# The x3 stage of a four-layer kernel: factor rows in two tiles, x2 loads issued behind the x3 store, gate product in the gate's tile

## Chip, cores and metric

The kernel runs on one core of a Trainium2 chip. The metric is the device time of one execution in microseconds (us); the kernel before took 3424.25 us, the median of 3 runs (3423.7 to 3426.99). PE is the engine for matrix products, DVE the vector engine, ACT the engine for functions, POOL the general one, SP the engine that issues most of the DMAs here.

## The reference, cut to what matters

Four layers act on an image of 256 x 256 tokens with 128 channels (D), each as x = x + layer(gn(x)). The change lies in the end of layer 2, the triangle multiplication. Cut to that:

```python
zn = layernorm(gn(x), ln_in_w, ln_in_b)
a = sigmoid(zn @ Wga + bga) * (zn @ Wla + bla)
b = sigmoid(zn @ Wgb + bgb) * (zn @ Wlb + blb)
k = einsum('bimc,bmjc->bijc', a, b)
out = sigmoid(zn @ Wgo + bgo) * (layernorm(k, ln_o_w, ln_o_b) @ Wlo + blo)
x3 = x + out
```

The group norm of layer 3 needs the sum and the sum of squares of each channel of x3, so these are taken on the way.

## The kernel before, in words

Data stays channel-major between the stages: x2T, kD and x3T are DRAM arrays of 128 rows (channels) by 65536 tokens. A chunk is SC = 2048 tokens, 1 MB in float32, and there are NSC = 32 chunks. Three stages bear on the change:

- The stage that makes a and b (L1101 to L1235) leaves the factor 1/sqrt(var + eps) of every token in rs2D, and the gates of the last two chunks (30 and 31) in tiles of their own, `gates`.
- The triangle product (L1257 to L1294) goes over the 128 channels in 32 groups of four. For each group SP issues the store of k, the loads of the next a and b, and in the last three groups a load of x2 (`load7x`, chunks 0 to 2).
- The x3 stage (L1300 to L1398) goes over the 32 chunks. The order of its instructions on every engine is the order of the program (`manual_schedule`).

One step s of the x3 stage, as it is written:

- `load7k(s + 3)` (L1309): the load of k for chunk s + 3 into one of 4 tiles.
- `load7x(s + 5)` (L1254, L1255): the load of x2 for chunk s + 5 and of its factor row, 2048 numbers into one partition of the tile rs2. Seven tiles hold x2: three from one pool, four from another. Chunk s + 5 takes the tile of chunk s - 2, so its load waits until the x3 store of chunk s - 2 has landed. The row of chunk s takes partition 32 * (s % 4), so four rows are held.
- For each half h of 1024 tokens:
  - `gate7(s + 3, h)`: PE multiplies x2 by the gate's weight (L1329), DVE adds a column and multiplies by the broadcast factors into the tile p7_zg, of which there are two (L1339, "the gate product"), ACT takes the sigmoid into the gate tile p7_g, of which there are five (L1340). So chunk s + 3 uses the gate tile of chunk s - 2.
  - PE multiplies the normalised k by the output weight (L1329), and DVE adds a bias and multiplies by the gate, into the gate tile (L1383, "the second product").
  - In the first half PE spreads the factors of k for chunk s + 1 (L1087), and POOL broadcasts the factor row of chunk s + 4 to all partitions, into one of two tiles (`spread_z`, L1323).
  - DVE multiplies k of chunk s + 1 by its factors (L1318).
- POOL adds the product to x2, in the x2 tile (L1396). In the last chunk DVE does it (L1389).
- `finish7(s - 1)`: ACT takes the sum and the sum of squares of x3 of chunk s - 1 (L1343, L1344). Both write their full output, which nobody reads, into the gate tile of chunk s - 1. SP stores x3 (L1349).

The profile leaves digits out of names: p_x is p7_x, p_zg is p7_zg, p_g is p7_g, p_k is p7_k, p_rb is the broadcast factor, p_rk the spread factors of k, p_pm the PSUM tiles of the products, and rs__17908 the tile of the factor rows. A wait is set by the framework from the tiles: who first writes into a reused tile waits for the last users of what was there.

Of the kernel before, what the change touches and what calls it, by code (L numbers as in the profile page):

```python
# [9 lines left out]
F32 = mybir.dt.float32  # L10
AF = mybir.ActivationFunctionType
# [5 lines left out]
P = 128  # L17
# [3 lines left out]
SC = 2048  # L21
NSC = T // SC
# [10 lines left out]
def kernel(ctx: ExitStack, tc: tile.TileContext, a: dict, out: bass.AP):  # L33
    nc = tc.nc
# [22 lines left out]
    rs2D = dram.tile([1, T], F32, name="rs2D")  # L57
# [89 lines left out]
    b2w = const.tile([P, 6], F32, name="b2w")  # L147
# [91 lines left out]
    with tc.tile_pool(name="x0", bufs=1) as xres, tc.tile_pool(name="p0", bufs=3) as sb:  # L239
        held = {s: xres.tile([P, SC], F32, name=f"x0_{s}") for s in range(RES, NSC)}  # L240
        with tc.tile_pool(name="p0ps", bufs=3, space=PSUM) as ps, tc.tile_pool(
            name="f0ps", bufs=2, space=PSUM
# [167 lines left out]
        with tc.tile_pool(name="p1", bufs=2) as wk_sb, tc.tile_pool(  # L410
            name="p1ps", bufs=4, space=PSUM
# [70 lines left out]
    with tc.tile_pool(name="p2e", bufs=6) as eb, tc.tile_pool(name="p2c", bufs=1) as cs:  # L482
        triT = cs.tile([P, NH, 2, N], F32, name="triT")
        with tc.tile_pool(name="p2", bufs=2) as sb, tc.tile_pool(
            name="p2S", bufs=2, space=PSUM
        ) as psS, tc.tile_pool(name="p2z", bufs=1, space=PSUM) as psZ, tc.tile_pool(
            name="p2M", bufs=3, space=PSUM
# [361 lines left out]
    with x1_scope:  # L849
        with tc.tile_pool(name="p3", bufs=3) as sb, tc.tile_pool(  # L850
            name="p3ps", bufs=3, space=PSUM
# [41 lines left out]
        with tc.tile_pool(name="z", bufs=2) as sb, tc.tile_pool(  # L893
            name="zps", bufs=3, space=PSUM
# [28 lines left out]
            at = turn_z(0)  # L923
            for k in range(16):
                nxt = turn_z(k + 1)
                pz = tri_multiply(nc, ps, at, AB[k // 2][1], k % 2).rearrange("p t n -> p (t n)")
                at = nxt
# [32 lines left out]
        with tc.tile_pool(name="p4", bufs=3) as sb, tc.tile_pool(  # L960
            name="p4psg", bufs=2, space=PSUM
        ) as psg, tc.tile_pool(name="p4psz", bufs=2, space=PSUM) as psz, tc.manual_schedule():
            zs, gts, sums = {}, {}, []
# [42 lines left out]
            for i, s in enumerate(order):  # L1006
# [14 lines left out]
                for h in range(2):  # L1021
                    hs = slice(h * 2 * CK, (h + 1) * 2 * CK)
# [57 lines left out]
    H2 = 2 * CK  # L1080
# [157 lines left out]
    rk_pool = rs2_scope.enter_context(tc.tile_pool(name="rk", bufs=1))  # L1238
    x7_pool = rs2_scope.enter_context(tc.tile_pool(name="x7", bufs=3))
    rk = rk_pool.tile([P, CK], F32, name="rk")  # L1240
    rs2 = rk_pool.tile([P, SC], F32, name="rs2_")

    def row7(s):
        at = 32 * (s % 4)
        return rs2[at : at + 1, :]

    k1 = rk_pool.tile([P, 2 * N], F32, name="k1")
    k2 = rk_pool.tile([P, 2 * N], F32, name="k2")
# [2 lines left out]
    def load7x(s, pool, bufs):  # L1251
        if s < NSC:
            xs7[s] = pool.tile([P, SC], F32, name="p7_x", bufs=bufs)
            nc.sync.dma_start(xs7[s], x2T[:, s * SC : (s + 1) * SC])  # L1254
            nc.sync.dma_start(row7(s), rs2D[:, s * SC : (s + 1) * SC])  # L1255

    with tc.tile_pool(name="p6", bufs=3) as sb, tc.tile_pool(name="p6ps", bufs=3, space=PSUM) as ps:  # L1257
        nc.vector.memset(k1, 0.0)
        nc.gpsimd.memset(k2, 0.0)  # L1259
        with tc.manual_schedule():  # L1260
            quads = {}

            def load6(q):
                if q < D // 4:
                    A = sb.tile([P, 4, 2 * N], F32, name="p6_A")
                    nc.sync.dma_start(A, aD[:, 4 * q : 4 * q + 4, :])
                    B = sb.tile([P, 4, 2 * N], F32, name="p6_B")
                    nc.sync.dma_start(B, bD[:, 4 * q : 4 * q + 4, :])
                    quads[q] = A, B

            def turn6(c):
                return tri_turn(nc, ps, sb, quads[c // 4][0], c % 4, ident, nc.vector.tensor_copy)

            for q in range(3):
                load6(q)
            at = turn6(0)
            for c in range(D):
                q = c // 4
                if c % 4 == 0:
                    K = sb.tile([P, 4, 2 * N], F32, name="p6_K")  # L1280
                nxt = turn6(c + 1) if c + 1 < D else None
                pz = tri_multiply(nc, ps, at, quads[q][1], c % 4).rearrange("p t n -> p (t n)")
                at = nxt
                nc.scalar.copy(K[:, c % 4, :], pz)  # L1284
                sq = sb.tile([P, 2 * N], F32, name="p6_sq")
                nc.scalar.activation(sq, pz, AF.Square)  # L1286
                nc.vector.tensor_tensor(k1, pz, k1, ALU.add)  # L1287
                nc.gpsimd.tensor_tensor(k2, k2, sq, ALU.add)  # L1288
                if c % 4 == 3:
                    nc.sync.dma_start(kD[4 * q : 4 * q + 4, :].rearrange("c (p t) -> p c t", p=P), K)  # L1290
                    del quads[q]
                    load6(q + 3)
                    if q >= D // 4 - 3:
                        load7x(q - (D // 4 - 3), x7_pool, 3)  # L1294
# [5 lines left out]
    with tc.tile_pool(name="p7", bufs=2) as sb, tc.tile_pool(name="p7psX", bufs=2, space=PSUM) as psX, tc.tile_pool(  # L1300
        name="p7psM", bufs=2, space=PSUM
    ) as psM, tc.manual_schedule():
        ks, rks, rbs, gts = {}, {}, {}, dict(gates)
        AHEAD = 3

        def load7k(s):
            if s < NSC:
                ks[s] = sb.tile([P, SC], F32, name="p7_k", bufs=4)
                nc.sync.dma_start(ks[s], kD[:, s * SC : (s + 1) * SC])  # L1309

        def spread_k(s):
            if s < NSC:
                rks[s] = broadcast_rows(psX, rk, s, "p7_rk")

        def normalise_k(s, h):
            if s < NSC:
                hs = slice(h * H2, (h + 1) * H2)
                nc.vector.tensor_tensor(ks[s][:, hs], rks[s][h], ks[s][:, hs], ALU.mult)  # L1318

        def spread_z(s):  # L1320
            if s < NSC and s not in gates:
                rbs[s] = sb.tile([P, SC], F32, name="p7_rb")
                nc.gpsimd.partition_broadcast(rbs[s], row7(s))  # L1323

        def product7(src, w, h):
            pm = psM.tile([P, 2, CK], F32, name="p7_pm")
            for c in range(2):
                k = 2 * h + c
                nc.tensor.matmul(pm[:, c, :], lhsT=w, rhs=src[:, k * CK : (k + 1) * CK], start=True, stop=True)  # L1329
            return pm.rearrange("p c t -> p (c t)")  # L1330

        def gate7(s, h):
            if s < NSC and s not in gates:
                hs = slice(h * H2, (h + 1) * H2)
                if h == 0:
                    gts[s] = sb.tile([P, SC], F32, name="p7_g", bufs=5)
                pg = product7(xs7[s], wf2[:, 4, :], h)
                zg = sb.tile([P, H2], F32, name="p7_zg")
                nc.vector.scalar_tensor_tensor(zg, pg, gcol, rbs[s][:, hs], ALU.add, ALU.mult)  # L1339
                nc.scalar.activation(gts[s][:, hs], zg, AF.Sigmoid, bias=b2w[:, 4:5])  # L1340

        def sums7(x, junk, i):
            nc.scalar.activation(junk, x, AF.Identity, bias=m2neg, accum_out=g1[:, i : i + 1])  # L1343
            nc.scalar.activation(junk, x, AF.Square, bias=m2neg, accum_out=g2[:, i : i + 1])  # L1344

        def finish7(s):
            x = xs7.pop(s)
            sums7(x, gts.pop(s), s)
            nc.sync.dma_start(x3T[:, s * SC : (s + 1) * SC], x)  # L1349

        load7k(0)
        load7x(3, sb, 4)
        spread_z(0)
        spread_z(1)

        nc.vector.scalar_tensor_tensor(k1, k1, -1.0 / D, k1, ALU.mult, ALU.mult)
        nc.vector.tensor_tensor(k2, k2, k1, ALU.add)
        nc.vector.tensor_scalar(k2, k2, 0.0, None, ALU.max)
        nc.scalar.activation(k2, k2, AF.Sqrt, bias=epst, scale=1.0 / D)
        nc.vector.reciprocal(k1, k2)  # L1360
        nc.sync.dma_start(rkD.rearrange("o (p t) -> p (o t)", p=P), k1)
        for c in range(4):
            nc.sync.dma_start(rk[32 * c : 32 * c + 32, :], rkD.rearrange("o (s c t) -> c (o s) t", c=4, t=CK)[c])
        for s in range(1, 3):
            load7k(s)
        load7x(4, sb, 4)
        for s in range(3):
            gate7(s, 0)
            gate7(s, 1)
            if s < 2:  # L1370
                spread_z(s + 2)
        spread_k(0)
        normalise_k(0, 0)
        normalise_k(0, 1)
        for s in range(NSC):
            load7k(s + 3)
            load7x(s + 5, *((x7_pool, 3) if (s + 5) % 7 < 3 else (sb, 4)))
            last = s == NSC - 1
            for h in range(2):
                hs = slice(h * H2, (h + 1) * H2)  # L1380
                gate7(s + AHEAD, h)
                pl = product7(ks[s], w2[:, 5, :], h)
                nc.vector.scalar_tensor_tensor(gts[s][:, hs], pl, b2w[:, 5:6], gts[s][:, hs], ALU.add, ALU.mult)  # L1383
                if h == 0:
                    spread_k(s + 1)
                    spread_z(s + AHEAD + 1)
                normalise_k(s + 1, h)
                if last:
                    nc.vector.tensor_tensor(xs7[s][:, hs], xs7[s][:, hs], gts[s][:, hs], ALU.add)  # L1389
                    if h == 0:  # L1390
                        finish7(s - 1)
                    sums7(xs7[s][:, hs], gts[s][:, hs], s + h)
                    nc.sync.dma_start(x3T[:, s * SC + h * H2 : s * SC + (h + 1) * H2], xs7[s][:, hs])
            del ks[s]
            if not last:
                nc.gpsimd.tensor_tensor(xs7[s], xs7[s], gts[s], ALU.add)  # L1396
                if s:
                    finish7(s - 1)  # L1398

# [483 lines left out]
```

## Time and profile before

| what | value |
|---|---|
| median of 3 runs | 3424.25 us |
| the profiled execution, device time | 3423.35 us |
| its span, first to last instruction | 3421.6 us |
| mean granted PE clock | 0.956 |
| triangle product, 2349 to 2640 us | 291 us, PE busy 289.81 |
| x3 stage up to its first store, 2640.0 to 2674.4 us | 34.4 us, PE busy 28.71, DMA 345 GB/s |
| x3 stage, first steps, 2674.4 to 2701.2 us | 26.8 us, PE busy 26.80, DMA 316 GB/s |
| x3 stage, further steps, 2701.2 to 2958.5 us | 257.3 us, PE busy 204.72, DVE 166.38, ACT 144.18, POOL 150.53, DMA 271 GB/s |
| x3 stage, last steps without gates, 2958.5 to 2997.5 us | 39.0 us, PE busy 22.96 |

The span is the time from the first to the last instruction; some 1.75 us of the device time lie outside of it. "Busy" is the time in which an engine worked; a clock of 1.00 is full speed. A group line shows who wrote what from what, the busy time of the group, the mean of one instruction, and then the idle time of that engine just before it with what ended that idle time. A wait line names the waiting instruction, then what ended its wait. Lines with SPq are DMA issues by SP.

### The profile page before, as it was taken

The page shows a single profiled execution, that of the slowest core. Times are in us where ns is not written, and L with a number is a line of the kernel's source. Part 1 is how long each engine was busy: PE and PEld are TensorE (multiplying, and loading weights), DVE is VectorE, ACT ScalarE, POOL GpSimd, SP SyncE. Part 2 cuts the span into 40 slices and gives each one's busy share as a digit, 9 for nine tenths or more (in the row PEclk, how much of TensorE's full clock was granted, in tenths as well). Part 3 has the DMA queues.
Part 4 walks back from the last instruction along what each step waited for, and adds up shares of the span by engine and source line. Part 5 has one row for each costly group of instructions (what it writes and reads, how often), then busy time and mean ns, then how long its engine had stood idle before and what let it go on. Part 6 is the DMA issues. An engine that isn't in the chain of part 4 may idle for free. (4 is left out here: it accounts for less than half of the span.)

```text
span 3421.6 us, 52156 instructions
## 1 busy us (share of the span) xinstructions
PE 3105.4 (91%) x20036; PEld 1648.5 (48%) x20036; DVE 2273.1 (66%) x2613; ACT 2021.0 (59%) x2209; POOL 1659.4 (48%) x904
## 2 busy tenths in 40 slices
PE   5669999999999999967996999999999987759998
PEld 5415555555555555524332444446997332224444
DVE  5627888888888888853555444554555766647776
ACT  3566777777777777734685454443444555626665
POOL 4045777777777777711581000002555655513443
PEclk7889999999999999989998999999999999979999
DMA  9982333333333333378697676767998877756764
GB/s 359 353 312 91 108 120 108 118 115 110 119 107 119 109 122 107 107 308 313 232 403 287 233 301 270 257 246 273 351 351 330 303 270 276 279 163 195 206 198 134
DMA packets 297913, 749.50 MB, mean 219 GB/s; under 512 B 74553, under 2 KB 145163, under 8 KB 248475
## 3 DMA queue, kind: packets, MB, share of 16 engines
q1 hardware_dynamic: 289723, 735.50, 60.4%
q0 software_dynamic: 7648, 9.55, 0.8%
q8 instruction: 161, 2.64, 0.3%
q10 hardware_dynamic: 288, 1.05, 0.1%
q14 instruction: 93, 0.76, 0.1%
HBM read 458.35 MB, written 287.64 MB: 218 GB/s over the span
## 5 line engine op out<-in xcount | busy, mean ns | idle before, releaser
L565 DVE TENSOR_TENSOR p_e<-p_S,triT 128x1024 f32<-128x1024 f32 x512 | 609.5, 1212 | 144.2 <-PE p_S L555 144.2
L575 POOL TENSOR_TENSOR p_es<-p_e 128x1024 f32<-128x1024 f32 x256 | 603.7, 2372 | 123.9 <-issue 65.1
L573 ACT ACTIVATE p_e<-p_e,mbT 128x1024 f32<-128x1024 f32 x512 | 552.0, 1138 | 59.8 <-DVE p_e L565 59.7
L1172 PE MATMUL p_pm<-p_zn,wf 128*128 128x512 f32 x1040 | 449.1, 593 | 2.2 <-ACT p_a L1207 1.9
L540 PE MATMUL p_mm<-p_xn,w 128*128 128x512 f32 x768 | 404.7, 610 | 0.3 <-DVE p_v L535 0.3
L1172 PEld LDWEIGHTS p_pm<-p_zn,wf 128*128 128x128 f32 x1040 | 196.7, 190 | 254.7 <-issue 246.5
L555 PE MATMUL p_S<-p_q,p_k 32*128 32x256 f32 x4096 | 294.9, 400 | 3.5 <-DVE p_e L565 3.3
L1579 POOL TENSOR_TENSOR p_q<-p_q,p_pb 128x2024 f32<-128x2024 f32 x32 | 144.1, 4503 | 252.0 <-DVE p_pb L1573 243.5
L555 PEld LDWEIGHTS p_S<-p_q,p_k 32*128 32x128 f32 x4096 | 185.7, 184 | 159.5 <-PE p_mm L531 91.7
L1843 PE MATMUL tp_z<-p_B,tp_at 128*128 128x256 f32 x1024 | 250.7, 388 | 0.7 <-DMA p_B<-bD 0.5
L514 POOL TENSOR_TENSOR p_xn<-p_xn,p_rs 128x1024 f32<-128x1024 f32 x63 | 151.2, 2400 | 204.9 <-DMA p_rb<-rzD 114.1
L588 PE MATMUL p_o<-p_e,p_v 128*32 128x256 f32 x4096 | 247.6, 382 | 0.0
L1259 POOL MEMSET k<- 128x512 f32 x1 | 0.5, 519 | 504.9 <-DVE p_zn L1165 504.9
L1288 POOL TENSOR_TENSOR k<-k,p_sq 128x512 f32<-128x512 f32 x128 | 162.9, 1273 | 159.1 <-ACT p_sq L1286 159.1
L1843 PEld LDWEIGHTS tp_z<-p_B,tp_at 128*128 128x128 f32 x1024 | 185.1, 191 | 22.6 <-DVE tp_at L1834 1.5
L1329 PE MATMUL p_pm<-p_x,wf 128*128 128x512 f32 x240 | 131.2, 677 | 58.8 <-DMA p_x<-x2T 52.6
L540 PEld LDWEIGHTS p_mm<-p_xn,w 128*128 128x128 f32 x768 | 125.8, 190 | 104.1 <-issue 88.1
L1287 DVE TENSOR_TENSOR k<-tp_z,k 128x512 f32<-128x512 f32 x128 | 88.5, 692 | 126.8 <-ACT p_sq L1286 126.8
L588 PEld LDWEIGHTS p_o<-p_e,p_v 128*32 128x32 f32 x4096 | 120.0, 109 | 109.3 <-ACT p_g L546 41.5
L1284 ACT COPY p_K<-tp_z 128x512 f32<-128x512 f32 x128 | 74.9, 585 | 157.6 <-PE tp_z L1843 157.6
L546 ACT ACTIVATE p_g<-p_mm,bgh 128x512 f32<-128x512 f32 x128 | 87.9, 687 | 131.3 <-PE p_mm L540 131.2
L531 PEld LDWEIGHTS p_mm<-w,p_xn 128*128 128x128 f32 x1024 | 134.4, 191 | 61.1 <-issue 60.4
(380 smaller groups left out, 5966.4 us busy)
## 6 DMA issues: line engine op xcount, KB each, us to landing
p_x<-x2T SPq DMA_DIRECT2D x60, 1024.0 KB
x<-x1T SPq DMA_DIRECT2D x51, 1024.0 KB
p_x<-in_x_dram SPq DMA_DIRECT2D x32, 1024.0 KB
p_x<-xT SPq DMA_DIRECT2D x64, 512.0 KB
x2T<-x SPq DMA_DIRECT2D x32, 1024.0 KB
aD<-p_a SPq DMA_DIRECT2D x32, 1024.0 KB
bD<-p_b SPq DMA_DIRECT2D x32, 1024.0 KB
p_A<-aD SPq DMA_DIRECT2D x32, 1024.0 KB
```

The lines of the kernel that those rows point to most:

```text
L514: nc.gpsimd.tensor_tensor(xn, xn, groups[g]["rs"], ALU.mult)
L531: nc.tensor.matmul(pm[:, k * D : (k + 1) * D], lhsT=t["xn"][:, b * P : (b + 1) * P], rhs=wf[:, 2 * D : 3 * D], start=True, stop=True,)
L540: nc.tensor.matmul(pm, lhsT=w, rhs=t["xn"][:, cs_], start=True, stop=True)
L555: nc.tensor.matmul(Ss[h // 2][:, h % 2, u, :], lhsT=t["k"][hp, r * N + u * P : r * N + (u + 1) * P], rhs=t["q"][hp, r * N : (r + 1) * N], ...
L565: nc.vector.tensor_tensor(e[:, :, 2 * p : 2 * p + 2, :].rearrange("p u h n -> p h u n"), Ss[p], triT[:, 2 * p : 2 * p + 2, :, :], ALU.add,)
L573: nc.scalar.activation(e[:, u, :, :], e[:, u, :, :], AF.Exp, bias=mbT[:, u, i : i + 1])
L575: nc.gpsimd.tensor_tensor(es, e[:, 0, :, :], e[:, 1, :, :], ALU.add)
L588: nc.tensor.matmul(t["o"][hp, r % 2, :], lhsT=t["v"][:, r * 2 + u, hp], rhs=e[:, u, h, :], start=(u == 0), stop=(u == 1),)
L1172: nc.tensor.matmul(pm[:, c, :], lhsT=wf2[:, i, :], rhs=zns[s][:, k * CK : (k + 1) * CK], start=True, stop=True)
L1288: nc.gpsimd.tensor_tensor(k2, k2, sq, ALU.add)
L1579: nc.gpsimd.tensor_tensor(q[:, :, 1 : N - 2], q[:, :, 1 : N - 2], pb[:, :, 0 : N - 3], ALU.add)
L1843: nc.tensor.matmul(pz[:, t, :], lhsT=at[:, u, t * P : (t + 1) * P], rhs=Bc[:, u, :], start=(u == 0), stop=(u == 1))
```

## The change

It has three parts, all of them in the x3 stage:

1. The factor rows get two tiles instead of one, so eight rows are held. Their loads are taken out of `load7x` and made by `load_row7`: rows 0 to 5 at the start of the triangle product, then row s + 6 at the start of step s. Rows of the chunks 30 and 31, whose gates exist already, are no longer loaded.
2. The x2 load of chunk s + 5 is issued at the end of step s, behind the x3 store of chunk s - 1. Before, it was issued near the step's start, in front of that store.
3. The gate product is written into the gate tile, and ACT takes the sigmoid in place. The tiles p7_zg are gone.

```diff
-    rs2 = rk_pool.tile([P, SC], F32, name="rs2_")
+    rs2 = [rk_pool.tile([P, SC], F32, name=f"rs2_{i}") for i in range(2)]
     def row7(s):
         at = 32 * (s % 4)
-        return rs2[at : at + 1, :]
+        return rs2[s // 4 % 2][at : at + 1, :]
+
+    def load_row7(s):
+        if s < NSC - 2:
+            nc.sync.dma_start(row7(s), rs2D[:, s * SC : (s + 1) * SC])
...
             xs7[s] = pool.tile([P, SC], F32, name="p7_x", bufs=bufs)
             nc.sync.dma_start(xs7[s], x2T[:, s * SC : (s + 1) * SC])
-            nc.sync.dma_start(row7(s), rs2D[:, s * SC : (s + 1) * SC])
...
             for q in range(3):
                 load6(q)
+            for s in range(6):
+                load_row7(s)
...
                 pg = product7(xs7[s], wf2[:, 4, :], h)
-                zg = sb.tile([P, H2], F32, name="p7_zg")
+                zg = gts[s][:, hs]
                 nc.vector.scalar_tensor_tensor(zg, pg, gcol, rbs[s][:, hs], ALU.add, ALU.mult)
-                nc.scalar.activation(gts[s][:, hs], zg, AF.Sigmoid, bias=b2w[:, 4:5])
+                nc.scalar.activation(zg, zg, AF.Sigmoid, bias=b2w[:, 4:5])
...
         for s in range(NSC):
+            load_row7(s + 6)
             load7k(s + 3)
-            load7x(s + 5, *((x7_pool, 3) if (s + 5) % 7 < 3 else (sb, 4)))
             last = s == NSC - 1
...
                 nc.gpsimd.tensor_tensor(xs7[s], xs7[s], gts[s], ALU.add)
                 if s:
                     finish7(s - 1)
+            load7x(s + 5, *((x7_pool, 3) if (s + 5) % 7 < 3 else (sb, 4)))
```

## The prediction

> **What bounds the kernel now.** First the page, its chain that ended last, by line:
>
> ```profile
> PE p_pm L1172 13%; PE tp_z L1843 7%; DMA x3T<-p_x 5%; PE p_pm L1565 5%; PE p_pm L1329 2%; PE tp_a L1832 2%; PE p_st L1129 2%; PE p_pt L1602 1%; DMA p_x<-x2T 1%; PE p_eb L1087 1%; DMA p_er<-eD 1%; DMA p_t<-tD 1%; DMA p_x<-x3T 1%; PE p_pp L1458 1%; DMA x2T<-x 1%
> ```
>
> The third item is a store of the x3 stage: the chain runs through stores for 5% of the span. Next, the waits of SP's DMA queue (2600 to 3010 us) and of the engines (2640 to 3000 us); columns are total us, times, longest:
>
> ```profile
> SPq L1254 <- DMA x3T<-p_x: 235.5, 25, 10.6
> SPq L1349 <- POOL p_x L1396: 27.0, 9, 7.4
> ```
>
> ```profile
> ACT p_g L1340 <- DVE p_zg L1339: 136.5, 52, 4.7
> POOL p_rb L1323 <- DMA rs__17908<-rs2D: 62.2, 14, 6.1
> PE p_pm L1329 <- DMA p_x<-x2T: 52.6, 21, 3.6
> ```
>
> SP stands 235.5 us in front of the x2 load, waiting for a store to land. The timeline of the stage shows the loop:
>
> ```profile
> 2782.73 0.32 SPq L1254 DMA_DIRECT2D p_x<-x2T  x1
> 2783.10 0.28 SPq L1255 DMA_DIRECT2D rs__17908<-rs2D  x1
> 2783.43 0.32 SPq L1349 DMA_DIRECT2D x3T<-p_x  x1
> 2783.86 0.36 SPq L1309 DMA_DIRECT2D p_k<-kD  x1
> 2794.49 0.32 SPq L1254 DMA_DIRECT2D p_x<-x2T  x1
> ```
>
> Seven x tiles rotate, so the load of chunk s+5 needs the store of chunk s-2 landed, and that store was issued just ahead of it. One step is one store's flight (2783.43 to 2794.49, 11.06) plus 0.7 of issue. The stores issued from 2701.87 to 2959.21 are 22 periods of 11.70 us. No engine is full: windows of the triangle product stage and of these steps, columns after the length PE, PEld, DVE, ACT, POOL busy, clock, DMA share, GB/s:
>
> ```profile
> 2349.00:2640.00 291.00, 289.81 (x1533) 261.45 (x1531) 164.48 (x255) 138.22 (x255) 161.69 (x127) 0.99 0.92 344
> ...
> 2701.20:2958.50 257.30, 204.72 (x542) 77.41 (x541) 166.38 (x136) 144.18 (x136) 150.53 (x44) 0.93 0.78 271
> ```
>
> DMA moved 344 GB/s before, 271 here: latency bounds, not bandwidth.
>
> **What the Trainium skill says.** "DMA: Bandwidth & Descriptors", section "Issuing engines are not separate DMA queues": all DMAs run on the same 16 engines and interleave. The trace agrees: a 1 MB load and a 1 MB store issued 0.7 us apart take 9.4 (2782.73 to the matmul at 2792.09) and 11.1. "TensorE: Matmul & The Clock Gate", "Part 1: The HAM clock gate": the PE falls to half clock after an idle window of about 3.4 us; its section "Why this matters for your kernels" asks for no gaps over about 3 us. The trace agrees roughly (below). Same page, "Architectural detail": ACT and DVE are strict FIFO; no engine here overtakes in the trace either.
>
> **Part 1: x2 load behind the store.** On SP's queue the x load is moved past the row load, the k load and the store of chunk s-1. The k load waits for a k tile that PE frees at the end of step s-1 (SP waited 12.9 us for PE at L1309 in all), the store for the POOL add of chunk s-1 (the 27.0 above); both become the waits in front of the load. The load still needs store s-2, but that was issued a whole step earlier: two stores may fly at once, and the 11.06 us are spread over two steps, 5.5 each, no longer the bound. What is late next: the load itself, see the slack below, and else the engines. One x3 step then needs the busiest resource: PE 8.14 us (zg at 2683.06 to zg at 2691.20, below, with PE gapless), DMA 3.146 MB at 344 GB/s = 9.14, POOL 2.29 + 4.55.
>
> **Part 2: rows.** 30 row loads of 8 KB instead of 32, six issued early in a stage whose PE is 99.6% busy: cost 0. POOL's 62.2 us of row waits go; its adds were ahead of the stores that SP held back, so 0 is gained. If that cover goes, POOL has 6.84 us of work in a step and still fits.
>
> **Part 3: no zg tile. Here a wait is added.** The five gate tiles rotate: chunk t+4's is that of t-1, whose last user is the second sum (L1344), writing it as junk. Before, only ACT wrote first into a new gate tile (sigmoid, behind its own sums: free). Now DVE's gate product writes first, so in step t+1 it waits for ACT to end the sums of chunk t-1. The instruction order of the changed kernel confirms it: from chunk 5 on the first gate product carries a wait on ACT. Behind it on DVE queue the second product (L1383), the k normalisation (L1318) and the next gate product; PE waits for those to free PSUM. An undisturbed step of before (start, duration):
>
> ```profile
> 2684.38 1.15 ACT L1340 ACTIVATE p_g<-p_zg,b2w 128x1024 f32<-128x1024 f32 x1 [1.69 <-DVE p_zg L1339]
> ...
> 2689.46 0.19 ACT L1344 ACTIVATION_READ_ACCUMULATOR p_g<-p_x,m2neg 128x1 f32 x1
> ```
>
> ```profile
> 2683.06 1.28 DVE L1339 SCALAR_TENSOR_TENSOR p_zg<-p_pm,gcol,p_rb 128x1024 f32<-128x1024 f32 x1 [0.56 <-PE p_pm L1329]
> ...
> 2687.04 1.28 DVE L1339 SCALAR_TENSOR_TENSOR p_zg<-p_pm,gcol,p_rb 128x1024 f32<-128x1024 f32 x1
> 2688.24 1.28 DVE L1383 SCALAR_TENSOR_TENSOR p_g<-p_pm,b2w,p_g 128x1024 f32<-128x1024 f32 x1
> 2689.43 1.22 DVE L1318 TENSOR_TENSOR p_k<-p_rk,p_k 128x1024 f32<-128x1024 f32 x1
> 2691.20 1.28 DVE L1339 SCALAR_TENSOR_TENSOR p_zg<-p_pm,gcol,p_rb 128x1024 f32<-128x1024 f32 x1 [0.56 <-PE p_pm L1329]
> ```
>
> The gate product at 2687.04 would wait until 2689.65; its size stays 128x1024 f32, so its duration too. The closed loop, from one second-half gate product to the next: product 1.28 + 0.04 to ACT; sigmoid start to end of sums 2684.38 to 2689.65 = 5.27; 0.05 to DVE (0.04 seen at L1405); then first-half product, second product, normalisation back to back, 1.20 + 1.20 + 1.13 = 3.53 (starts at 2687.04, 2688.24, 2689.43; 1.13 from other back-to-back pairs). Sum **10.17 us per step**. PE can't shorten it: its next gate matmuls start 1.33 into that 3.53 and need 2.09 to the product, 3.42. The trace shows no DVE wait for this line, so I bound it: 0.1 less if ACT signals at the end of the square (0.19 of reading the sum follow it) and the hand-overs are shorter, 0.2 more if each of the three costs 0.1 rather than 0.04: 10.0 to 10.4. So 10.17 exceeds PE's 8.14 and DMA's 9.14 (3.146 MB per 10.17 is 309 GB/s) and replaces 11.70, but also the 8.13 of the first steps.
>
> **Slack of the late load.** Call Z the first gate product of a step. The POOL add ends at Z + 3.53 + 1.65 + 1.28 + 0.16 + 4.55 = Z + 11.2, 1.0 into the next step; there store, then x load, at 1.9 at the latest (store flight 11.06 against a step of 10.17). It lands 9.4 later, 1.1 into the step after; PE wants it at 4.9 (second-half gate matmuls at 1.35, the next first-half ones 3.54 behind, as from 2680.97 to 2684.51 in PE's timeline). Slack 3.8 us, cost 0; bounds 0 to +0.3 us a step if loads take 12 to 13.
>
> **Sum.** Before, Z of step 2 is 2678.91 and Z of step 26 (chunk 29, last with such a gate) 2947.93. After, Z of step 2 waits for the sums ending 2681.51: 2681.56. 24 steps x 10.17 = 244.1, Z of step 26 at 2925.6: -22.3. Tail: in step 26 PE was slow after a wait (4.82 instead of 3.53 between products, 1.3), and the k load of the last chunk came late (adds of POOL 7.8 apart instead of 5.6, 2.2), issued behind the waiting x loads; now k loads are issued up to a step earlier: -3, bounds -3.5 and 0. Total -25.3. The profiled execution took 3423.35 (span 3421.6); less 25.3 is 3398. The median, 0.9 above it, gives **3399**. With 10.0 to 10.4 per step and the tail's bounds: 3394 to 3408.
>
> **Clock.** PE idles 10.17 - 8.14 = 2.03 a step. Restarts of before (gap in brackets):
>
> ```profile
> 2734.68 1.95 PE L1329 MATMUL p_pm<-p_x,wf 128*128 128x512 f32 x4 [1.94 <-DMA p_x<-x2T]
> ...
> 2932.73 1.96 PE L1329 MATMUL p_pm<-p_x,wf 128*128 128x512 f32 x4 [1.99 <-DMA p_x<-x2T]
> ```
>
> All nine gaps up to 1.99 restart at full speed (1.95), ten of the twelve from 2.19 up (after 3.55: 3.65) do not. I take full speed; it is near the edge.
>
> **Rivals.**
> - Slower: PE restarts cold. If 2.03 us are too long, the four gate matmuls inside the loop take 3.5 instead of 1.95: 11.72 per step, step 26 at 2962.8, +14.9 - 3: **3436**. Break-even is 11.2 per step. For: 2.19 was slow. Against: nine gaps. Chance 0.13.
> - Half: every other restart is cold, or loads use up their slack: 10.95 per step, -3.6 - 3: **3418**. Chance 0.11.
> - Not as it says: the added wait is for something earlier (the sigmoid, say) and DMA bounds at 9.14: 2678.91 + 219.4 = 2898.3, -49.6 - 3: **3372**. For: more in flight. Against: the rotation of five. Chance 0.06.
> - Forecast: 0.70.
>
> **Chances and range.** 0.2% (7 us) is about what can be told from no change. Faster: forecast and DMA-bound, 0.76; same: half, 0.11; slower: 0.13. Leaving out the DMA-bound and the cold case keeps 0.81: 3393 to 3420; the forecast's own 3394 to 3408.
>
> **What would show it.** SP's wait of L1254 for x3T falls from 235.5 to under 50; POOL's for rows to near 0; DVE's gate product waits for ACT's L1344 line some 2.5 us in 25 steps; steps 10.2 apart; PE gaps near 2.0, restarting at 1.95. Wrong if steps are 9 or 11.7 apart, or if PE still waits for x2 loads over 20 us in total.

## The result, and the profile after

The changed kernel takes 3402.82 us (median of 4 runs, 3396.51 to 3407.79) against 3423.97 us before (4 runs, 3422.72 to 3426.99): ratio 0.9936, 95% interval 0.9915 to 0.9957. It is faster by 21 us, clear of noise though only 0.6%; 25 were forecast. The profiled execution is the longest of the four, 3407.79 us with a span of 3405.9. Line numbers from 1249 on differ from those of before by up to 6: the row load is now L1249, the x2 load L1258, the k load L1314, the normalisation of k L1323, the matmuls L1334, the gate product L1344, its sigmoid L1345, the sums L1348 and L1349, the x3 store L1354, the second product L1388, the POOL add L1401.

The chain that ended last, by line, as the page gives it:

```profile
PE p_pm L1172 13%; PE tp_z L1849 7%; PE p_pm L1571 4%; PE tp_a L1838 2%; PE p_st L1129 2%; PE p_pm L1334 2%; ACT p_g L1349 1%; ACT p_g L1348 1%; DMA p_x<-x3T 1%; DVE p_g L1344 1%; PE p_pt L1608 1%; DVE p_g L1388 1%; ACT p_g L1345 1%; DMA p_t<-tD 1%; PE p_eb L1087 1%
```

The 5% of "DMA x3T<-p_x", the store in the chain of before, is gone. In its place stand PE's L1334, both sums, the gate product, the sigmoid and the second product: the members of the loop that the prediction closed. SP's waits (2600 to 3010 us) and the engines' waits (2640 to 3000 us) after; the columns are total us, times, longest:

```profile
SPq L1354 <- POOL p_x L1401: 173.9, 31, 5.8
SPq L1314 <- PE p_pm L1334: 69.3, 27, 5.8
```

```profile
ACT p_g L1345 <- DVE p_g L1344: 115.7, 59, 3.9
...
DVE p_g L1344 <- ACT p_g L1349: 67.3, 25, 3.0
...
PE p_pm L1334 <- DVE p_g L1344: 51.8, 26, 4.0
```

SP no longer waits for a store to land (235.5 us before). It waits for POOL's add and for PE, since it is early. PE's 52.6 us for x2 loads and POOL's 62.2 us for rows are gone (one wait of 5.0 us is left on POOL). New is DVE's wait for the second sum, 25 times 2.69 us. The timeline of DVE shows one step, from one such wait to the next:

```profile
2722.86 1.28 DVE L1344 SCALAR_TENSOR_TENSOR p_g<-p_pm,gcol,p_rb 128x1024 f32<-128x1024 f32 x1 [2.69 <-ACT p_g L1349]
2724.06 1.28 DVE L1388 SCALAR_TENSOR_TENSOR p_g<-p_pm,b2w,p_g 128x1024 f32<-128x1024 f32 x1
2725.25 1.22 DVE L1323 TENSOR_TENSOR p_k<-p_rk,p_k 128x1024 f32<-128x1024 f32 x1
2726.38 1.28 DVE L1344 SCALAR_TENSOR_TENSOR p_g<-p_pm,gcol,p_rb 128x1024 f32<-128x1024 f32 x1
...
2733.04 1.28 DVE L1344 SCALAR_TENSOR_TENSOR p_g<-p_pm,gcol,p_rb 128x1024 f32<-128x1024 f32 x1 [2.69 <-ACT p_g L1349]
```

2722.86 to 2733.04 is 10.18 us, where before had 11.70. The window of these steps (columns after the length: PE, PEld, DVE, ACT, POOL busy, clock, DMA share, GB/s):

```profile
2701.20:2940.50 239.30, 195.30 (x562) 75.05 (x560) 170.14 (x142) 148.97 (x141) 156.76 (x47) 0.99 0.84 306
```

No engine is full here either. What bounds is now a loop over DVE and ACT, no longer a transfer.

**Where the time came from.** The first read of x3 by the next stage is issued at 2997.53 us before and at 2974.12 after: 23.4 us earlier. From there to the end of the span it is 424.1 us before and 431.8 after, so the two profiled executions as a whole differ by only 15.6. The code of that last stage is the same in all kernels here, and over the fourteen profiles of this case it takes from 421 to 432 us; before is near the low end, after at the high one. What makes that spread stays open. The medians do not show a loss there: the unaltered kernel run again (e1_again below) gave 0.9925.

### The profile page after: what moved, and what is told of

The parts are those of the page before. It is cut to its first block, busy times and chain, and to the rows that moved or that the text cites. A ratio compares the mean times of both kernels' runs of the same rounds, so it can differ in the third digit from the quotient of the medians.

```text
span 3405.9 us, 52131 instructions
## 1 busy us (share of the span) xinstructions
PE 3094.3 (91%) x20036; PEld 1645.1 (48%) x20036; DVE 2269.6 (67%) x2613; ACT 2021.2 (59%) x2209; POOL 1659.1 (49%) x904
## 3 DMA queue, kind: packets, MB, share of 16 engines
q10 hardware_dynamic: 288, 1.05, 0.1%
## 5 line engine op out<-in xcount | busy, mean ns | idle before, releaser
L1401 POOL TENSOR_TENSOR p_x<-p_x,p_g 128x2048 f32<-128x2048 f32 x30 | 136.0, 4535 | 97.9 <-ACT p_g L1345 59.2
L1334 PE MATMUL p_pm<-p_x,wf 128*128 128x512 f32 x240 | 121.7, 634 | 53.7 <-DVE p_g L1344 51.8
```

## The experiments

The parts are numbered here as in "The change": 1 is the rows, 2 the x2 load behind the store, 3 the gate product in the gate's tile. (The prediction calls the x2 load Part 1 and the rows Part 2.) Where rows are loaded at the start of a step but the second tile of rows is left out, they are loaded five chunks ahead.

**The changed kernel again, unaltered (e1_again).**

> The changed kernel unaltered, to see how far its last stage (from the first x3 read to the end) varies: it took 431.8 us in the profile after and 424.1 in the one before. If the longer last stage belongs to the change: again near 432. If it is chance of how its small transfers fall: other values between 420 and 433 here, and times spread from 3396 to 3408 as before. The x3 stage itself should repeat to 0.5 us: steps of 10.18.

3403.25 us (6 runs, 3396.79 to 3407.05), ratio 0.9925 [0.9911, 0.994]; steps of 10.18 us. The last stage took 430.2 us in the profile, within its usual spread. All ten executions of this kernel lie between 3396.5 and 3407.8.

**Part 3 alone (e2_part3_alone).** The kernel before with

```diff
-                zg = sb.tile([P, H2], F32, name="p7_zg")
+                zg = gts[s][:, hs]
...
-                nc.scalar.activation(gts[s][:, hs], zg, AF.Sigmoid, bias=b2w[:, 4:5])
+                nc.scalar.activation(zg, zg, AF.Sigmoid, bias=b2w[:, 4:5])
```

> The kernel before with part 3 alone (gate product in the gate's tile). My theory: two separate loops, of which the longer one rules, ACT's sums to DVE (10.18 us) and the store's flight (11.7 us). From the third step on the first steps take 10.18 instead of 8.13 until the store loop takes over at the third store, so +2 us in all, 3424 to 3428, with DVE waiting for ACT's sums in the early steps and for the x2 load later. Rival: the two waits add up in every step, 11.7 + 2 us, over 24 steps some +48: 3472.

3424.48 us (16 runs), ratio 0.9978 [0.9962, 0.9993]. But the runs are spread from 3396.58 to 3431.99: four of sixteen lie below 3410. The profiled one is the longest; SP waits 234.6 us for x3 stores as before, and steps are about 11.7 us. None of the 23 runs of before beside them is below 3420. So part 3's wait alone costs next to nothing, and in some executions it comes with a gain; e6 and e12 below show how.

**Part 2 alone (e3_part2_alone).** The kernel before with the x2 load behind the store, and the row load at the start of the step; p7_zg stays:

```diff
...
         for s in range(NSC):
+            load_row7(s + 5)
             load7k(s + 3)
-            load7x(s + 5, *((x7_pool, 3) if (s + 5) % 7 < 3 else (sb, 4)))
...
                     finish7(s - 1)
+            load7x(s + 5, *((x7_pool, 3) if (s + 5) % 7 < 3 else (sb, 4)))
```

> The kernel before with part 2 alone: the x2 load behind the x3 store, the row load at the start of the step five chunks ahead in the one tile, gate product in its own tile p7_zg. My theory: without part 3's wait the step falls to what DMA needs for 3.146 MB, 9.14 us at 344 GB/s, not to 10.18; the x3 stage ends some 53 us earlier than before: 3371, or 3347 if DMA keeps up with PE's 8.14. Rival (10.18 comes from something else, such as PE or the load's place): 3399 to 3405 as with the whole change.

3350.91 us (4 runs, 3345.45 to 3353.16), ratio 0.9771 [0.9753, 0.979]: 52 us below the whole change. Its window:

```profile
2677.50:2888.90 211.40, 211.40 (x623) 82.54 (x622) 186.76 (x156) 164.72 (x155) 175.84 (x51) 1.00 1.00 386
```

PE is busy 211.40 of 211.40 us: it is the bound, with steps of 8.13 us. And DMA moves 386 GB/s, where the prediction took 344 as what it can give. SP waits for no x3 store in these steps, although the transfers of a step go out close together:

```profile
2701.90 0.32 SPq L1354 DMA_DIRECT2D x3T<-p_x  x1
2702.32 0.37 SPq L1258 DMA_DIRECT2D p_x<-x2T  x1
...
2704.01 0.57 SPq L1314 DMA_DIRECT2D p_k<-kD  x1
2709.97 0.32 SPq L1354 DMA_DIRECT2D x3T<-p_x  x1
```

**The whole change without the wait (e4_sums_early).** The sums and the store of chunk s - 1 are moved from the end of step s into its first half:

```diff
                 if h == 0:
+                    if s and not last:
+                        finish7(s - 1)
                     spread_k(s + 1)
...
-                if s:
-                    finish7(s - 1)
```

> The changed kernel with the sums and the store of chunk s-1 moved from the end of step s to the middle of it, between the two halves, so that ACT ends the sums some 4 us before DVE needs the gate tile. My theory: the wait of DVE for the sums goes to near 0 and the step falls to DMA's 9.14 us: 3371 (3347 if PE's 8.14 rules). Rival (the wait is moved to ACT's second sigmoid, which then stands behind the sums, and from there to the second product): 3395 to 3405.

3352.47 us (5 runs, 3342.98 to 3353.26), ratio 0.9768 [0.9751, 0.9785]; PE is again busy 211.40 of 211.40 us, steps 8.13. All three parts are in, but the sums end early enough that DVE no longer waits for them: its waits for L1349 are gone from the profile. (The store moves forward with them; that SP is not the bound at 10.18 is seen in its own waits above, and the next kernel prolongs the loop alone.)

**The second sum twice (e9_sum_twice).** The changed kernel with a longer stay of ACT in the loop:

```diff
             nc.scalar.activation(junk, x, AF.Square, bias=m2neg, accum_out=g2[:, i : i + 1])
+            nc.scalar.activation(junk, x, AF.Square, bias=m2neg, accum_out=g2[:, i : i + 1])
```

> The changed kernel with ScalarE's second sum done twice in every step, same result. If DVE's first gate product, waiting for that sum, closes the loop that sets the step, the added sum (about 2.1 us) goes onto every step: 10.18 becomes about 12.3 us, the x3 stage ends about 50 us later, total near 3453 us. Rival, the loop is not what sets 10.18 (a transfer or SP sets it): ScalarE has idle time in each step and takes the sum there; the steps lengthen by less than 1 us, total under 3430 us.

3501.03 us in a single run, where 3453 was expected: the step grows by more than the added sum. Timeline of DVE, then of PE:

```profile
2768.55 1.28 DVE L1344 SCALAR_TENSOR_TENSOR p_g<-p_pm,gcol,p_rb 128x1024 f32<-128x1024 f32 x1 [4.67 <-ACT p_g L1350]
...
2782.21 1.28 DVE L1344 SCALAR_TENSOR_TENSOR p_g<-p_pm,gcol,p_rb 128x1024 f32<-128x1024 f32 x1 [4.67 <-ACT p_g L1350]
```

```profile
2769.89 3.47 PE L1334 MATMUL p_pm<-p_x,wf 128*128 128x512 f32 x4 [3.96 <-DVE p_g L1344]
...
2783.55 3.47 PE L1334 MATMUL p_pm<-p_x,wf 128*128 128x512 f32 x4 [3.96 <-DVE p_g L1344]
```

A step is 13.66 us, 3.48 more. The sigmoid's start to the end of the sums is 7.40 instead of 5.27 (+2.13). The rest is PE: its gap grows from 1.90 to 3.96, all nineteen restarts (the four matmuls behind such a gap) from 2701 to 2948 us are slow (3.44 to 3.68 for four matmuls instead of 1.98), and these matmuls now lie on the loop: from DVE's first gate product to its second it is 4.84 instead of 3.52 (+1.32). The two add up to 3.45 of the 3.48. That is the mechanism of the prediction's slower rival, seen at a gap of 4 us.

**Part 1 alone (e7_part1_alone).** The kernel before with the row load in front of the k load; the x2 load stays in front of the store.

```diff
...
         for s in range(NSC):
+            load_row7(s + 5)
             load7k(s + 3)
```

> The kernel before with the row load alone moved, to the start of the step in front of the k and x2 loads (five ahead, one tile). POOL's waits for rows should go from 62 us to near 0 and the time stay where it was, 3420 to 3432, since POOL has slack. Rival (POOL's row wait was part of the loop, through the add that the store needs): 3400 or less.

3432.2 us in a single run (before, run beside it, 3426.98); steps 11.7 to 11.8, SP waits 239.7 us for stores. POOL's waits for rows are gone and nothing is gained.

**Parts 1 and 3, x2 load in front of the store (e6_parts13, e12_parts13_again).** The changed kernel with part 2 undone:

```diff
             load7k(s + 3)
+            load7x(s + 5, *((x7_pool, 3) if (s + 5) % 7 < 3 else (sb, 4)))
...
                     finish7(s - 1)
-            load7x(s + 5, *((x7_pool, 3) if (s + 5) % 7 < 3 else (sb, 4)))
```

> The changed kernel with part 2 undone: rows in two tiles and gate product in the gate's tile stay, the x2 load stands again in front of the x3 store. My theory: the store's flight rules again, steps of 11.7 us and 3424 to 3432, as with part 3 alone. Rival (the early rows are what brought the gain): 3400 to 3405.

That missed: 3404.83 us in a single run, with steps of 10.19 as in the whole change. From this one run I took it that beside part 3 the place of the x2 load is worth nothing, and formed a second theory: the 11 us flight of a store (the time from its issue to its landing) is not a property of the store, but of what is issued with it. When SP is late, x load, row, store and k load are all ready and go out within 1.1 us; they share the DMA engines, the store lands late, and SP is late again. I call this a burst that keeps itself going. A slower pace of the engines would spread the issues and dissolve it. This kernel was run again (e12); e13, e10 and e11 each change something that the theory turns on.

> The changed kernel with the x2 load back in front of the x3 store, as looked at once before (3404.83 us, steps of 10.18 us), now in several executions. Two things differ between it and the kernel with the gate product in the gate's tile alone, which is near 3424 us in most executions: the place of the factor row's load on SP (here behind the store, there between the x2 load and the store), and chance. If the row's place decides, all executions lie near 3399 to 3408 us. If it was chance, most lie near 3424 us and a few near 3404 us, as in the other.

3421.13 us (12 runs), ratio 0.9969 [0.9947, 0.9991]; the runs go from 3402.28 to 3436.88, seven of twelve are over 3410. So the single run was one of the good ones. The profiled execution (3409.11) holds both behaviours, one after the other. SP's timeline:

```profile
2802.16 0.32 SPq L1258 DMA_DIRECT2D p_x<-x2T  x1
2803.19 0.32 SPq L1354 DMA_DIRECT2D x3T<-p_x  x1
...
2807.30 0.32 SPq L1314 DMA_DIRECT2D p_k<-kD  x1
2812.39 0.32 SPq L1258 DMA_DIRECT2D p_x<-x2T  x1
2813.37 0.32 SPq L1354 DMA_DIRECT2D x3T<-p_x  x1
...
2817.48 0.32 SPq L1314 DMA_DIRECT2D p_k<-kD  x1
2824.14 0.32 SPq L1258 DMA_DIRECT2D p_x<-x2T  x1
...
2847.52 0.32 SPq L1258 DMA_DIRECT2D p_x<-x2T  x1
2847.90 0.42 SPq L1354 DMA_DIRECT2D x3T<-p_x  x1
...
2848.76 0.32 SPq L1314 DMA_DIRECT2D p_k<-kD  x1
2859.38 0.32 SPq L1258 DMA_DIRECT2D p_x<-x2T  x1
```

Up to 2812 the x loads are 10.19 us apart and the k load follows the store by 4.1. Then one store, issued at 2813.37, is not landed before 2824.14, and from there on the x loads are 11.6 to 12.0 apart; within three steps the k load follows the store by 0.86. It does not come back. Windows and SP's waits of the two stretches (the first pair of waits from 2690 us on):

```profile
2700.00:2810.00 110.00, 89.28 (x255) 34.70 (x256) 79.34 (x66) 67.91 (x63) 72.62 (x23) 1.00 0.92 308
2836.00:2941.00 105.00, 85.33 (x237) 32.55 (x236) 71.79 (x60) 62.65 (x59) 62.87 (x19) 0.97 0.77 270
```

```profile
SPq L1258 <- DMA x3T<-p_x: 42.4, 12, 4.7
...
SPq L1258 <- ACT p_g L1349: 15.5, 12, 1.6
```

```profile
SPq L1258 <- DMA x3T<-p_x: 81.0, 8, 10.5
```

In the first stretch (the upper pair) the store has landed 1.3 us (15.5 / 12) before the load's other wait, for ACT, is over: that is the margin. In the burst the wait for the store is 10.1 us a step. What delayed the one store at 2813 stays open, and so does what starts the burst in the kernel before.

**The row's place (e13_row_behind).** Part 3 alone, with the row load moved from between x2 load and store to behind the store:

```diff
             nc.sync.dma_start(xs7[s], x2T[:, s * SC : (s + 1) * SC])
-            nc.sync.dma_start(row7(s), rs2D[:, s * SC : (s + 1) * SC])
...
                     finish7(s - 1)
+            load_row7(s + 5)
```

> The kernel before with the gate product in the gate's tile, and with one row load moved: the factor row of chunk s + 5 is issued behind the x3 store of chunk s - 1 at the end of the step, no longer between the x2 load and that store; x2 load and the one tile of rows stay. Theory A, that a row load in front of the store is what lets the burst form at a pace of 10.18 us: no execution bursts, all near 3399 to 3408 us. Theory B, that the row has no part: most executions near 3424 us, some near 3404 us.

Four runs: 3399.97, 3400.87, 3418.8, 3427.67 us (ratio 0.9929 [0.99, 0.9957]); the last, profiled, bursts from 2689 us on. Theory A falls: a row behind the store doesn't keep the burst away. Whether it makes it rarer, four runs can't tell.

**More work for PE (e10_more_pe).** The kernel before, with the matmuls that spread the factors of k done three times from chunk 2 on:

```diff
...
-                rks[s] = broadcast_rows(psX, rk, s, "p7_rk")
+                rb = [psX.tile([P, 2, CK], F32, name="p7_rk", tag="x") for _ in range(2)]
+                for c in (0, 1, 2, 3) * (3 if s > 1 else 1):
...
```

> The kernel before, with the matmuls that spread the k factors done three times from chunk 2 on (same result): TensorE's own work in a step rises from about 8.13 to about 10.27 us, nothing else changes. Theory that the 11.70 us step of the kernel before is a burst that keeps itself going (a late SP issues x load, row, store and k load together, they share the DMA engines, the store lands late, SP is late again): a TensorE that paces the steps at 10.3 lets SP come early, its issues are spread out, the store's flight falls below the step, and the kernel is FASTER for the added work: steps near 10.3 us, total about 3400 to 3406 us. Rival, the store's flight of about 11 us is fixed by its size and bounds the step whatever TensorE does: steps stay at 11.7 us, total 3424 to 3432 us.

3403.35 us (5 runs, 3400.64 to 3417.68), ratio 0.9937 [0.9917, 0.9958]: the kernel before becomes faster, by as much as the whole change brought, for work that is of no use. Its window and SP's wait for stores show why:

```profile
2701.20:2940.00 238.80, 238.80 (x980) 96.72 (x972) 175.37 (x145) 154.78 (x147) 161.80 (x47) 1.00 0.92 320
```

```profile
SPq L1254 <- DMA x3T<-p_x: 83.2, 25, 3.8
```

PE is gapless and paces the steps at 9.85 us (my 10.27 for it was 0.4 too high); SP's wait at L1254 for stores falls from 235.5 to 83.2 us. The issues are spread: the k load follows the store by 3.7 to 3.8 us (2782.31 to 2786.05, 2792.09 to 2795.91), not by 0.4. A fixed flight of 11 us is excluded.

**Without the k loads (e11_no_k).** The kernel before, leaving out the loads of k from chunk 4 on (older k tiles are used again):

```diff
...
+                if s > 3:
+                    ks[s] = ks4[s % 4]
+                    return
...
```

> The kernel before, leaving out the k loads of all chunks but the first four (later chunks use those tiles again, so the k values of the output are not the reference's): 2 MB instead of 3 MB move in a step, and the order on SP is that of the kernel before. Theory that the store's flight is set by what is issued beside it: without the k load it falls from 11.06 to about 8 us or less, steps become about 8.2 to 8.8 us, total about 3350 to 3365 us. Rival, the flight belongs to the store itself: it stays near 11 us and the steps near 11.7 us, total 3424 to 3432 us.

3361.51 us in a single run. SP's timeline:

```profile
2761.02 0.32 SPq L1353 DMA_DIRECT2D x3T<-p_x  x1
2769.34 0.32 SPq L1254 DMA_DIRECT2D p_x<-x2T  x1
...
2770.09 0.32 SPq L1353 DMA_DIRECT2D x3T<-p_x  x1
2778.32 0.32 SPq L1254 DMA_DIRECT2D p_x<-x2T  x1
```

Without 1.05 MB of load issued behind it, the same store takes 8.3 us (2761.02 to 2769.34, 2770.09 to 2778.32), not 11.06, and the step is 9.05 (8.2 to 8.8 were expected). From these two flights I estimate the flight in a burst as about 2.7 us plus 2.8 for each of the three transfers (11.06 - 8.28 = 2.78 for 1.05 MB, 377 GB/s): the bytes at full rate, and some 2.7 us in which little is moved. The trace of before agrees. In the period shown in the prediction DMA moves 117 GB/s from 2783.22 to 2785.18, 367 from there to 2793.02, and 33 from there to the next load at 2794.49; against 367 the two slow ends lose 1.3 us each, 2.7 in all. In the burst they lie open in each step, since nothing is queued while SP waits. The closeness of the issues alone is not the harm: in e3 store, x2 load and k load go out within 2.1 us, but SP waits for no store there, and DMA moves 386 GB/s.

**Less work for PE (e8_less_pe).** The kernel e4_sums_early, leaving out the spreading of the k factors for all chunks but the first:

```diff
...
-                rks[s] = broadcast_rows(psX, rk, s, "p7_rk")
+                rks[s] = rks[0] if s else broadcast_rows(psX, rk, s, "p7_rk")
```

> The kernel with the early sums (e4), leaving out the spreading of k's factors for all chunks but the first (the output is not the reference's): PE has 1.07 us less in a step, 7.06 instead of 8.13, DVE some 7.1, POOL 6.84, ACT 6.7. If PE alone bounds there: steps of 7.1 to 7.3, 26 to 33 us less than e4. If DMA, whose share was 1.00 at 387 GB/s, is at its limit as well: steps stay at 8.0 to 8.13.

3330.39 us in a single run:

```profile
2680.00:2850.00 170.00, 158.72 (x351) 62.89 (x350) 158.39 (x132) 139.94 (x132) 149.53 (x45) 1.00 1.01 405
```

PE falls to 158.72 of 170.00 us and DMA reaches 405 GB/s at a share of 1.01; steps are about 7.7 to 7.8, between the two that were expected. What DMA needs for a step lies there or below, not at 9.14.

## Why the prediction was right, point by point

- **What bounds before: right in what it shows, too narrow in why.** SP does wait for a store; but 11.06 us is what a store takes in a burst that keeps itself going. By the estimate under e11, "latency bounds, not bandwidth" holds for 2.7 us of it.
- **x2 load behind the store: right.** It takes the store of a step ago off the path. With the rows' loads moved but without part 3 it gives PE's 8.13 (e3). Beside part 3 it keeps all ten executions below 3408 us; without it seven of twelve are over 3410 (e12). Its slack held: PE waits for no x2 load.
- **Rows, cost and gain 0: right** (e7, a single run with one tile of rows).
- **Added wait, 10.17 us per step: right**, 10.18 measured; e4 takes it away and e9 prolongs it. The first gate product of step 2 was forecast at 2681.56 and came at 2681.77. That of step 26 was forecast at 2925.6 and came at 2928.07: one step of 11.69 (+1.5, the slow restart of PE shown below) and one of 10.54 (+0.4) are in it; the rest is the start (+0.2) and 24 x 0.013.
- **Tail, -3: right.** From that product to the first x3 read it is 49.60 before, 46.05 after: -3.55.
- **Clock: right, and near the edge as said.** PE's 25 restarts came behind gaps of 1.83 to 2.25 us, and 24 of them were at full speed. The other one, with its neighbour:

```profile
2866.79 1.98 PE L1334 MATMUL p_pm<-p_x,wf 128*128 128x512 f32 x4 [1.90 <-DVE p_g L1344]
...
2876.98 3.64 PE L1334 MATMUL p_pm<-p_x,wf 128*128 128x512 f32 x4 [1.90 <-DVE p_g L1344]
```

In the profile of e1_again the slow one is the same step (2877.86); why that one stays open. "The trace agrees roughly" with an idle window of about 3.4 us was too kind: in the profile of before ten of the twelve gaps from 2.19 us up restarted slowly, and only four of these twelve were above 3.4. The measured gaps count here.

- **Sum.** Forecast -25.3, at the first x3 read -23.4: 2.5 too little up to step 26, 0.55 more in the tail. The forecast of 3399 lies 4 us under the median, inside the spread of the runs.
- **Wrong, without harm to the number: "DMA bounds at 9.14 (3.146 MB at 344 GB/s)".** 344 GB/s was taken from a stage that PE bounds (289.81 of 291.00 us busy): it is what that stage asked for. DMA gives 386 to 405 (e3, e8). So the rival "DMA bounds", 3372, had the wrong price: without the added wait it is PE's 8.13 and 3351. Since 10.17 is above both floors, the forecast didn't feel it; but the added wait costs 2.05 us a step, twice the 1.03 that the prediction implied (10.17 less 9.14).

## What to carry to other kernels

A period in which a queue waits for its own last transfer can be a burst that sustains itself: before pricing its removal, see whether the queue stands empty during the wait, and what the flight is when fewer transfers go out with it. A bandwidth read from a stage that another engine bounds is a demand and no ceiling. When a change merges two tiles, see who now writes first into a reused one; here the merge cost 52 us of the 77 that moving the x2 load (with the rows' loads) had won (e3 against e1), and an earlier place of the two sums (e4) gave them back.

## What had not been expected of the hardware

- Work of no use on PE made the kernel faster by 0.6% (e10), by slowing the pace that had kept the transfers bunched.
- A store of 1 MB took 11.06 us with three transfers in a burst and 8.3 with two; spread out, it had landed about 7.9 us after its issue (e12's first stretch: 9.2 from store to next load, less the margin of 1.3).
- The two paces can follow each other in one execution, and a single execution (e6) told the wrong story.
- Gaps of about 1.9 us on PE restarted slowly once in 25 times, in the same step of both profiles of the changed kernel; gaps of 3.9 to 4.3 nineteen times in nineteen.
